# The last stage of a four-layer image kernel: its last block but one first, the last block stored in parts, and a fixed order

## The chip, the cores and the metric

The kernel runs on one core of a Trainium2 chip. The metric is the device time of one execution in microseconds (us), the median of three runs. The core has a matrix engine (TensorE, PE in the profile) with its weight loads (PEld), a vector engine (VectorE, DVE), a scalar engine (ScalarE, ACT), GpSimd (POOL) and a sync engine (SyncE, SP). Transfers between DRAM and the on-chip memory are issued as instructions of SP, ACT or POOL and carried out by 16 DMA engines. Each engine takes its instructions in the order in which they stand in its own queue; engines wait for each other, and for transfers, at semaphores.

## The reference

The input is an array of 8 images of 32 channels of 256 by 256, float32. Four layers follow each other, each of the form `x = x + layer(group_norm(x))`: a spectral convolution (FFT, 32 by 32 low modes mixed, inverse FFT), a 5 by 5 convolution, a gated recurrence over columns, and a mixing of directional maxima. The change touches the last two:

```python
# layer 2: a scan over the 256 columns; prev is the new column before, cur this column
r = sigmoid(r_i + r_h); z = sigmoid(z_i + z_h); n = tanh(n_i + r * n_h)
new = n * z + cur * (1.0 - z)
# layer 3: running maxima from four sides, then one matrix over 5*32 channels
x_con = concatenate((x, cummax_down, cummax_up, cummax_right, cummax_left), axis=1)
out = einsum('bchw,oc->bohw', x_con, W) + b
```

`_gn` ahead of each layer needs the mean and variance over a whole image, so layer 3's scales are known only when the recurrence has ended. One of the four maxima runs against the direction of the recurrence, so layer 3 goes through the columns from the last to the first.

## The kernel before

The program is four stages, one function each. The first two (`forward_and_mix`, `inverse_and_conv`) do layers 0 and 1 and leave their result in DRAM as `x2d`.

**The recurrence** (`recurrence`, lines 684 to 906) works on 32 blocks of 8 columns. A column is done in two half steps (`step(w, x)`, x = 0 and 1), four images each, so that one half step's matrix products run while the other's gates are computed. A half step has its matmuls on PE (lines 753 and 761), three sigmoids and a tanh on ACT (828, 830, 831, 835), four operations on DVE (829, 834, 840 and 842, the last writes the new column `hs`), and two on POOL (837, `zm` times `cur`, and 843, which adds the new column to the raw block `xw`). Between line 835 and line 840 one piece of extra work on DVE is fitted in (line 839): a running maximum from the left (`fm`, line 864) or a statistic (`bst`, line 875). As soon as a block is ended its `xw` is stored to DRAM as `x3d` by eight DMAs of 256 KB from SP (`store`, line 849), and its `fm`, when the pieces are through, as `fwd` by eight more. The `fwd` of the last block, 31, is issued from POOL instead of SP. Each of these DMAs reads 32 partitions. At the end lines 902 to 906 turn the statistics into `mv3`.

**The last stage** (`maxima_and_mix`, lines 909 to 1059) first makes its constants: it turns `mv3` into scales (`finish_stats`, lines 63 to 71, with a power on POOL), scaled weights `wsc` (936, 938) and biases `bres` (961, 962), and fills `cuts` and `top` (967 to 972) and `wsum` (942 to 946). A scheduler places this part: the fills and `wsum`, which need no statistics, stand on DVE in block 2 of the recurrence. Then it goes through blocks 31 to 0 in an order written out by hand (`tc.manual_schedule`). For a block it loads `x3` (the `x3d` block, 2 MB) and `fw` (the `fwd` block, 2 MB) from SP (line 980), with two buffers each, one block ahead. DVE does seven operations of maxima within the columns (lines 1014 to 1026: `x`, `top`, the scans `dq` and `uq`, and three times `m`) and, between them, eight steps of the maximum from the right (`back(7)` to `back(0)`, line 1012), each from the one before, across blocks by way of `after`. PE mixes five sources into eight banks (`mix`, line 1043: x, fw, the `downs` made of `m` and `dq`, the `ups` made of `uq` and `m`, then `rv`), ACT adds the bias (1058) and stores each half block (1059). `m`, `dq` and `uq` have one buffer each.

Instructions of different stages share each engine's queue. A tile of the last stage that lies in on-chip memory used by the recurrence waits until that memory's last user there is done.

Of the kernel before, what the change touches and what calls it, by code (L numbers as in the profile page):

```python
# [9 lines left out]
F32 = mybir.dt.float32  # L10
# [6 lines left out]
P = 128  # L17
# [3 lines left out]
EPS = 1e-5  # L21
# [662 lines left out]
def recurrence(tc, k, d, x2d, x3d, fwd, stb, first, loaded, mean1, mv3):  # L684
# [10 lines left out]
    with ExitStack() as ctx:  # L695
        one = ctx.enter_context(tc.tile_pool(name="bc", bufs=1))
        blk = ctx.enter_context(tc.tile_pool(name="bb", bufs=2))
# [22 lines left out]
        def load(bi):  # L720
            if bi:
                t = blk.tile([P, B, WB, Q], F32, name=f"xw_{bi}", tag="xw", bufs=4)
                for b in range(B):
                    nc.sync.dma_start(out=t[:, b], in_=columns(x2d, b, bi * WB, (bi + 1) * WB))
            else:
                t = first
                nc.sync.dma_start(out=t[:, B - 1], in_=columns(x2d, B - 1, 0, 8))
            raws[bi] = t
            norms[bi] = blk.tile([P, B, WB, Q], F32, name=f"xn_{bi}", tag="xn")
# [119 lines left out]
        def store(bi, dst, t):  # L849

            for a in range(A):
                for b2 in range(2):
                    (nc.gpsimd if bi == NB - 1 and dst is fwd else nc.sync).dma_start(
                        out=dst[bi, :, a, b2].rearrange("(i c) n -> c i n", c=C),
                        in_=t[rows(a), 4 * b2 : 4 * b2 + 4].rearrange("p i w q -> p i (w q)"),
                    )
# [13 lines left out]
        def finish(bi):  # L870
            raw = raws[bi]
            store(bi, x3d, raw)
            for b in range(B):
                pieces[1].append(
                    lambda b=b: nc.vector.bn_stats(bst[:, b, bi, :], raw[:, b].rearrange("p w q -> p (w q)"))
                )

        with tc.manual_schedule(engines=None):
# [5 lines left out]
            for bi in range(NB):  # L884
                for wi in range(WB):
# [7 lines left out]
                    running(bi, wi)  # L893
                finish(bi)
# [4 lines left out]
        parts = bst.rearrange("p b n (h k) -> p b (n h) k", k=3)  # L899
        n = 2 * NB  # L900
        second = one.tile([P, B, n], F32, name="second")
        nc.vector.tensor_tensor(second, parts[:, :, :, 1], parts[:, :, :, 1], ALU.mult)
        nc.vector.scalar_tensor_tensor(second, parts[:, :, :, 2], n / float(W * Q), second, ALU.mult, ALU.add)
        nc.vector.tensor_reduce(mv3[:, :, 0], parts[:, :, :, 1], AX.X, ALU.add)
        nc.vector.tensor_reduce(mv3[:, :, 1], second, AX.X, ALU.add)
        nc.vector.tensor_scalar_mul(mv3, mv3, 1.0 / n)


def maxima_and_mix(tc, k, d, x3d, fwd, mv3, mean1, out):
# [4 lines left out]
    NB = W // WB  # L914
    with ExitStack() as ctx:
        one = ctx.enter_context(tc.tile_pool(name="cc", bufs=1))
        blk = ctx.enter_context(tc.tile_pool(name="cb", bufs=2))
        op = ctx.enter_context(tc.tile_pool(name="co", bufs=3))
        ps = ctx.enter_context(tc.tile_pool(name="cp", bufs=2, space=PSUM))
# [5 lines left out]


        sta, _ = finish_stats(tc, one, ps, k, mv3, B, k.pair, "c", "o1", 2)
        st = one.tile([P, 2, 2], F32, name="st3")
        for i in range(4):
            q = slice(32 * i, 32 * i + 32)  # L930
            nc.vector.tensor_copy(st[q], sta[q, i::4, :])
        shift = one.tile([P, 2], F32, name="shift3")
        nc.vector.scalar_tensor_tensor(shift, st[:, :, 0], -1.0, st[:, :, 1], ALU.mult, ALU.mult)
        wsc = one.tile([P, 2, 5, C], F32, name="wsc")
        for b2 in range(2):
            nc.vector.tensor_scalar_mul(wsc[:, b2], w3, st[:, b2, 1:2])

            nc.vector.tensor_tensor(wsc[:, b2, 0], wsc[:, b2, 0], k.ident32, ALU.add)


        wsum = one.tile([P, A, C], F32, name="wsum")
        nc.vector.tensor_tensor(wsum[:, 0], w3[:, 0], w3[:, 1], ALU.add)
        for t in range(2, 5):
            nc.vector.tensor_tensor(wsum[:, 0], wsum[:, 0], w3[:, t], ALU.add)
        for j in range(1, A):
            nc.vector.tensor_copy(wsum[:, j], wsum[:, 0])
        sel = one.tile([P, 2, 4], F32, name="sel")
        nc.vector.memset(sel, 0.0)
        for i in range(4):
            q = slice(32 * i, 32 * i + 32)  # L950
            nc.vector.tensor_copy(sel[q, :, i], shift[q])
        bp = ps.tile([P, 2, 4], F32, name="bp", tag="o0")
        nc.tensor.matmul(
            bp.rearrange("p b i -> p (b i)"),
            lhsT=wsum.rearrange("p j o -> p (j o)"),
            rhs=sel.rearrange("p b i -> p (b i)"),
            start=True,
            stop=True,
        )
        bres = one.tile([P, 2, 4], F32, name="bres")  # L960
        nc.vector.tensor_scalar_add(bres, bp, b3[:, 0:1])
        nc.vector.tensor_tensor(bres, bres, mean1.rearrange("p (b i) -> p b i", b=2), ALU.add)


        QP = Q + 2
        cuts = one.tile([P, 2, 2 * WB, QP], F32, name="cuts")
        nc.vector.memset(cuts, BIG)
        nc.vector.memset(cuts[:, 0, :, 0:1], -BIG)
        nc.vector.memset(cuts[:, 1, :, QP - 1 : QP], -BIG)
        cutf = cuts.rearrange("p s w q -> p s (w q)")  # L970
        top = one.tile([P, 2, WB, QP], F32, name="top")
        nc.vector.memset(top, -BIG)

        xs = {}

        def load(bi):

            for src, tag, n in ((x3d, "x3", A + 2), (fwd, "fw", A)):
                t = xs[bi, tag] = blk.tile([P, n, 2, WB, Q], F32, name=f"{tag}_{bi}", tag=tag)
                nc.sync.dma_start(out=t[:, 0:A].rearrange("p a b w q -> p (a b) (w q)"), in_=src[bi].rearrange("p a b n -> p (a b) n"))  # L980
# [10 lines left out]
        after = None  # L991
        with tc.manual_schedule(engines=None):
            load(NB - 1)
            for bi in range(NB - 1, -1, -1):
                if bi > 0:
                    load(bi - 1)
                xt, fw = xs.pop((bi, "x3")), xs.pop((bi, "fw"))
                rev = blk.tile([P, A, 2, WB, Q], F32, name=f"rv_{bi}", tag="rv")
                x = [xt[:, a] for a in range(A)]

                m = blk.tile([P, 6, 2, WB, Q], F32, name=f"m_{bi}", tag="m", bufs=1)
                dq = blk.tile([P, 2, WB, QP], F32, name=f"dq_{bi}", tag="dq", bufs=1)
                uq = blk.tile([P, 2, WB, QP], F32, name=f"uq_{bi}", tag="uq", bufs=1)
                tt = nc.vector.tensor_tensor
                df, uf, tf = (t.rearrange("p b w q -> p (b w q)") for t in (dq, uq, top))

                def back(w):
                    last = after if w == WB - 1 else rev[:, :, :, w + 1, :]
                    if last is None:
                        nc.vector.tensor_copy(rev[:, :, :, w, :], xt[:, 0:A, :, w, :])  # L1010
                    else:
                        tt(rev[:, :, :, w, :], last, xt[:, 0:A, :, w, :], ALU.max)  # L1012

                tt(flat(xt[:, A : A + 2]), flat(xt[:, 0:A:2]), flat(xt[:, 1:A:2]), ALU.max)
                back(7)
                tt(top[:, :, :, 1 : 1 + Q], xt[:, A], xt[:, A + 1], ALU.max)
                back(6)
                nc.vector.tensor_tensor_scan(df, cutf[:, 0], tf, -BIG, ALU.min, ALU.max)  # L1018
                back(5)
                nc.vector.tensor_tensor_scan(uf[:, ::-1], cutf[:, 1, ::-1], tf[:, ::-1], -BIG, ALU.min, ALU.max)  # L1020
                back(4)
                tt(rows_of(m[:, 2:4]), twice(dq[:, :, :, 0:Q]), rows_of(xt[:, 0 : A + 1 : A]), ALU.max)  # L1022
                back(3)
                tt(rows_of(m[:, 0:2]), twice(uq[:, :, :, 2 : 2 + Q]), rows_of(xt[:, A - 1 : A + 2 : 2]), ALU.max)  # L1024
                back(2)
                tt(flat(m[:, 4:6]), flat(m[:, 1:4:2]), flat(xt[:, 1:3]), ALU.max)  # L1026
                back(1)
                back(0)
                after = rev[:, :, :, 0, :]
                downs = [m[:, 2], m[:, 3], m[:, 5], dq[:, :, :, 1 : 1 + Q]]  # L1030
                ups = [uq[:, :, :, 1 : 1 + Q], m[:, 4], m[:, 1], m[:, 0]]

                fws, rvs = [fw[:, a] for a in range(A)], [rev[:, a] for a in range(A)]
                pts = [
                    [ps.tile([P, 2 * H], F32, name=f"o_{bi}_{b2}_{i}", tag=f"o{i}") for i in range(4)] for b2 in range(2)
                ]


                def mix(b2, t, src, first=False, last=False):
                    for j in range(A):  # L1040
                        for i in range(4):
                            q = slice(32 * i, 32 * i + 32)
                            nc.tensor.matmul(  # L1043
                                pts[b2][i][32 * j : 32 * j + 32].rearrange("p (w q) -> p w q", q=Q),
                                lhsT=wsc[q, b2, t, :],
                                rhs=src[j][q, b2],
# [153 lines left out]
```

## Time and profile before

| what | value |
|---|---|
| median of 3 runs | 3066.25 us (3065.99 to 3067.99) |
| the profiled execution's own time | 3069.01 us |
| its span, first to last instruction | 3067.2 us |
| busy share PE, DVE, ACT, POOL | 91%, 84%, 61%, 28% |
| mean granted TensorE clock | 0.956 |
| last `hs` of the recurrence starts | 2402.73 us |
| first DVE operation on block 31 of the last stage starts | 2431.40 us |

The times of the profile count from the start of the span. In the page's slices each digit is the busy share of an engine in one of 40 equal pieces of the span (76.7 us each), so the recurrence ends in the 32nd digit. A timeline row gives start and duration in us, engine, line, operation and tiles (written `out<-in`), and in brackets the idle time before it with what ended it. A windows row gives a stretch, its length, and for each engine the busy us and, in brackets, the number of instructions, then the granted clock, the share of time in which the DMA engines were busy, and GB/s.

### The profile page before, as it was taken

To read this page: it belongs to the slowest core of one execution; us is meant where nothing else is said; L and a number is where in the kernel's file an instruction comes from. 1 tells how busy PE (TensorE), PEld (TensorE's weight loads), DVE (VectorE), ACT (ScalarE), POOL (GpSimd) and SP (SyncE) were. 2 spreads that over 40 slices of the span, in tenths; PEclk is the share of its full clock that TensorE was granted. 3 is DMA by queue.
4 is the path that set the end of the run, shared out by engine and by line. 5 is a ranking of instruction groups with operands and counts; after the bars stand their busy time and mean duration, and the time that the engine had idled before them with its cause. 6 is when DMAs were issued, how large, how long until landed. Compare 5 with 4: busy or idle time off the path is not lost.

```text
span 3067.2 us, 111686 instructions
## 1 busy us (share of the span) xinstructions
PE 2796.5 (91%) x47736; PEld 1645.3 (54%) x47736; DVE 2585.2 (84%) x5178; ACT 1870.4 (61%) x4482; POOL 858.2 (28%) x1247
## 2 busy tenths in 40 slices
PE   7986799999999799999999999999999588888887
PEld 4665344444444466666666666666666233333333
DVE  5752587778888589999999999999999799999997
ACT  3432377676777578888888888888887222222222
POOL 0110011111111355555555555555555200000000
PEclk9985899999999899999999999999999799999998
DMA  9977577777775565667666676666764588888885
GB/s 385 392 283 222 154 230 225 218 224 219 231 221 165 146 148 139 142 158 167 148 142 141 154 167 151 144 142 149 167 157 115 180 327 329 328 330 329 330 327 226
DMA packets 468193, 655.69 MB, mean 214 GB/s; under 512 B 328784, under 2 KB 329696, under 8 KB 441456
## 3 DMA queue, kind: packets, MB, share of 16 engines
q1 hardware_dynamic: 407528, 487.89, 54.6%
q0 software_dynamic: 16784, 84.11, 8.4%
q10 hardware_dynamic: 43384, 76.55, 6.9%
q8 instruction: 374, 6.13, 0.8%
q14 instruction: 123, 1.01, 0.1%
HBM read 371.63 MB, written 272.63 MB: 210 GB/s over the span
## 4 chain that ended last, share of the span: by engine, by line
PE 69%; DVE 20%; DMA 5%; issue 3%; ACT 2%; SPq 0%; ACTq 0%; POOL 0%; DVEq 0%; POOLq 0%
PE r L753 14%; PE z L753 13%; PE vp L487 11%; PE ni L753 6%; PE nh L753 6%; PE up L418 4%; DVE rv L1012 4%; PE yp L131 3%; DMA spec<-smd 3%; DVE dq L1018 2%; DVE uq L1020 2%; DVE m L1026 2%; DVE m L1024 2%; DVE m L1022 2%; PE sp L158 2%
## 5 line engine op out<-in xcount | busy, mean ns | idle before, releaser
L761 PE MATMUL z<-hs,weights 64*64 64x256 f32 x4080 | 539.2, 382 | 0.0
L761 PE MATMUL ni<-hs,weights 64*64 64x256 f32 x4080 | 525.7, 375 | 0.0
L761 PE MATMUL r<-hs,weights 64*64 64x256 f32 x4080 | 525.0, 375 | 0.0
L843 POOL TENSOR_TENSOR xw<-xw,hs 128x256 f32<-128x256 f32 x496 | 340.2, 686 | 635.3 <-DVE hs L842 635.3
L1058 ACT ACTIVATE ot<-o,bres 128x512 f32<-128x512 f32 x256 | 155.1, 688 | 505.1 <-PE o L1043 489.7
L487 PE MATMUL vp<-x,c_conv 64*64 64x384 f32 (+5 forms) x4608 | 428.8, 491 | 4.9 <-DVE x L520 4.9
L520 DVE SCALAR_TENSOR_TENSOR x<-vp,r,x 128x128 f32<-128x128 f32 (+2 forms) x640 | 350.6, 563 | 87.9 <-PE vp L487 75.1
L837 POOL TENSOR_TENSOR a<-zm,xn 128x256 f32<-128x256 f32 x510 | 373.1, 732 | 7.0 <-ACT zm L830 6.7
L835 ACT ACTIVATE n<-n,bih 128x256 f32<-128x256 f32 x510 | 259.5, 509 | 186.4 <-DVE n L834 186.4
L1043 PE MATMUL o<-m,wsc 32*32 32x512 f32 x3072 | 228.8, 724 | 108.0 <-DVE m L1026 104.4
L753 PE MATMUL r<-hs,weights 64*64 64x256 f32 x2040 | 318.9, 389 | 4.4 <-DVE hs L842 3.4
L753 PE MATMUL z<-xn,weights 64*64 64x256 f32 x2040 | 305.8, 377 | 14.9 <-DMA xw<-x2d 14.9
L487 PEld LDWEIGHTS vp<-x,c_conv 64*64 64x64 f32 x4608 | 222.4, 132 | 180.0 <-issue 104.4
L753 PE MATMUL r<-xn,weights 64*64 64x256 f32 x2040 | 305.3, 376 | 2.1 <-ACT rs L828 2.1
L753 PE MATMUL nh<-xn,weights 64*64 64x256 f32 x2040 | 306.2, 377 | 0.0
L753 PE MATMUL z<-hs,weights 64*64 64x256 f32 x2040 | 305.3, 376 | 0.0
L753 PE MATMUL ni<-hs,weights 64*64 64x256 f32 x2040 | 305.1, 375 | 0.0
L733 ACT ACTIVATE xn<-xw,shift,turned 128x256 f32<-128x256 f32 x496 | 290.3, 586 | 0.0
L829 DVE SCALAR_TENSOR_TENSOR n<-nh,bhh,rs 128x256 f32<-128x256 f32 x510 | 246.2, 483 | 46.4 <-ACT rs L828 32.6
L761 PEld LDWEIGHTS ni<-hs,weights 64*64 64x64 f32 x4080 | 284.8, 133 | 0.3
L761 PEld LDWEIGHTS r<-hs,weights 64*64 64x64 f32 x4080 | 280.9, 131 | 0.2
L828 ACT ACTIVATE rs<-r,brz 128x256 f32<-128x256 f32 x510 | 241.7, 474 | 54.2 <-PE r L761 33.8
(162 smaller groups left out, 6230.3 us busy)
## 6 DMA issues: line engine op xcount, KB each, us to landing
xb<-in_xl_dram POOLq DMA_DIRECT2D x96, 768.0 KB, 7.6
xa<-in_xt_dram SPq DMA_DIRECT2D x64, 1024.0 KB
x<-x3d SPq DMA_DIRECT2D x32, 2048.0 KB
fw<-fwd SPq DMA_DIRECT2D x32, 2048.0 KB
out_dram<-ot ACTq DMA_DIRECT2D x64, 1024.0 KB
xw<-x2d SPq DMA_DIRECT2D x248, 256.0 KB
fwd<-fm SPq DMA_DIRECT2D x248, 256.0 KB
x3d<-xw SPq DMA_DIRECT2D x248, 256.0 KB
```

The costliest lines, as they stand in the source:

```text
L487: ins = nc.tensor.matmul(vps[bank][to, :, dst], lhsT=k.conv[r, P : P + 64] if kind == 2 else k.conv[r, o], rhs=pair_of(u, ch, g, lo, hi, s ...
L520: nc.vector.scalar_tensor_tensor(x, src[o], r1[rows, g : g + 1], x, ALU.mult, ALU.add, accum_out=s1[rows, 0, n, ch, g : g + 1])
L733: nc.scalar.activation(norms[bi][:, b, w], raws[bi][:, b, w], AF.Identity, bias=shift[:, b : b + 1], scale=sc[:, 1, b : b + 1])
L753: ins = nc.tensor.matmul(out[r], lhsT=weights[r, kind, gate, :], rhs=src[r], start=start, stop=stop)
L761: ins = nc.tensor.matmul(out[pairs[1 - i]], lhsT=weights[r, kind, gate, :], rhs=prev[r, :, q0 : q0 + Q], start=False, stop=stop,)
L828: rs = nc.scalar.activation(r, p["r"], AF.Sigmoid, bias=brz[:, 0:1])
L829: nc.vector.scalar_tensor_tensor(m, p["nh"], bhh[:, 2:3], r, ALU.add, ALU.mult)
L835: nc.scalar.activation(m, m, AF.Tanh, bias=bih[:, 2:3])
L837: product = nc.gpsimd.tensor_tensor(a, zm, cur, ALU.mult)
L843: nc.gpsimd.tensor_tensor(raw, raw, new, ALU.add)
L1043: nc.tensor.matmul(pts[b2][i][32 * j : 32 * j + 32].rearrange("p (w q) -> p w q", q=Q), lhsT=wsc[q, b2, t, :], rhs=src[j][q, b2], start=first,
L1058: nc.scalar.activation(ot[:, i], pts[b2][i], AF.Identity, bias=bres[:, b2, i : i + 1])
```

## The change

What it does, part by part:

1. **Last block but one first.** The last stage takes block 30's within-column maxima first, block 31's next. `load_x(30)` is issued by ACT's queue; every other load stays on SP. `known(bi)` (PE's first four sources) and `finish(bi)` (the fifth source, biases, stores) are now separate, and an explicit order of DVE's work for the two blocks is given; `m10` stands for the first maximum of block 30, `b07` for `back(7)` of block 31. The right-hand maximum still runs 31, then 30. A copy `edge` is added for block 29, since the `rv` of block 30 and 29 share a buffer.
2. **Pools.** `x3`, `rv` and the recurrence's `xw` get a pool per buffer, so that block 30's `x3` buffer can lie in memory that is free before the recurrence ends.
3. **Last block stored in three parts.** `x3d` of block 31 is stored as columns 0 to 3 after column 3, 4 and 5 after column 5, and 6 and 7 at the end: 24 DMAs instead of eight. `fwd` of block 31 is issued by SP behind them.
4. **No scheduling freedom.** The statistics and the constants stand in `manual_schedule`; the fills and `wsum` go from DVE to POOL (`constants`).

In the built program of the changed kernel the instructions stand as follows. On ACT, `load_x(30)` is behind the third sigmoid of half step (250, 0), column 250 and x = 0, and waits for the eight `x3d` stores of block 30. On DVE, `m10` is in half step (250, 1), right behind line 829's operation there, and waits for that load. On POOL, the fills stand between the last half step of column 15 and the product of (16, 0), and `wsum` between that product and the next addition. The rest of the order is that of the text below. On SP, `load_x(31)` and `load_f(30)` come behind all stores of block 31, then `load_f(31)`, then `load_x(29)`. `m02` waits for PE's last read of `dq` of block 30, `m03` for that of `uq`, `m04` for that of `m`; `load_x(29)` waits for `b10`.

```diff
@@ recurrence
-                t = blk.tile([P, B, WB, Q], F32, name=f"xw_{bi}", tag="xw", bufs=4)
+                t = xws[(bi - 1) % 4].tile([P, B, WB, Q], F32, name=f"xw_{bi}", tag="xw")
...
-        def store(bi, dst, t):
+        def store(bi, dst, t, lo=0, hi=WB):
...
-                    (nc.gpsimd if bi == NB - 1 and dst is fwd else nc.sync).dma_start(
-                        out=dst[bi, :, a, b2].rearrange("(i c) n -> c i n", c=C),
+                    nc.sync.dma_start(
+                        out=dst[bi, :, a, b2, lo * Q : hi * Q].rearrange("(i c) n -> c i n", c=C),
...
-            store(bi, x3d, raw)
+            store(bi, x3d, raw, 6 if bi == NB - 1 else 0)
...
+                    if bi == NB - 1 and wi in (3, 5):
+                        store(bi, x3d, raws[bi], wi - 3 if wi == 3 else 4, wi + 1)
@@ maxima_and_mix
+        def constants():
+            nc.gpsimd.memset(cuts, BIG)
...
+            nc.gpsimd.memset(top, -BIG)
+            nc.gpsimd.memset(sel, 0.0)
+            nc.gpsimd.tensor_tensor(wsum[:, 0], w3[:, 0], w3[:, 1], ALU.add)
...
+        def load_x(bi, queue):
+            xs[bi] = xps[slot(bi)].tile([P, A + 2, 2, WB, Q], F32, name=f"x3_{bi}", tag="x3")
+            queue.dma_start(
...
+        def back(bi, w):
+            if w == WB - 1:
+                if bi == NB - 3:
+                    nc.vector.tensor_copy(edge, rvs[bi + 1][:, :, :, 0, :])
...
+        with tc.manual_schedule(engines=None):
+            load_x(NB - 2, nc.scalar)
+            load_x(NB - 1, nc.sync)
+            constants()
+            sums()
+            order("m10")
+            variance()
+            order("m11 m12")
+            scales()
+            load_f(NB - 2)
+            load_f(NB - 1)
+            order("m13")
+            biases()
+            order("m14 m15 m16")
+            known(NB - 2)
+            order("m00 b07 m01 b06 b05 m02 b04 b03 m03 b02 b01 b00")
+            order("b17 b16 b15 b14 b13 b12 b11 b10")
+            finish(NB - 2)
+            load_x(NB - 3, nc.sync)
+            load_f(NB - 3)
+            order("m04 m05 m06")
+            known(NB - 1)
+            finish(NB - 1)
+            for bi in range(NB - 3, -1, -1):
...
```

From block 29 on, the order within a block is that of before.

## The prediction

> **What bounds the kernel now.** I read the page's slices first, then the chain of waits in order of time around the end of the recurrence, then timelines and windows there. Slices (DVE's busy tenths, then TensorE's granted clock):
>
> ```profile
> DVE  5752587778888589999999999999999799999997
> PEclk9985899999999899999999999999999799999998
> ```
>
> DVE is nearly full in the recurrence (digits 16 to 31) and in the last stage (33 to 40). Only the 32nd digit, the passage between them, has a hole. The chain of waits there:
>
> ```profile
> 2402.73 0.43 DVE hs L842
> ...
> 2410.59 12.31 DMA x3d<-xw
> 2423.11 8.07 DMA x<-x3d
> 2431.40 2.29 DVE x L1014
> ```
>
> The recurrence ends, the stores of block 31 take until 2423.11, its load until 2431.40, and only then DVE starts on the last stage. From then on DVE alone sets the pace, as the timeline of DVE shows for two blocks:
>
> ```profile
> 2450.52 2.29 DVE L1014 TENSOR_TENSOR x<-x 128x2048 f32<-128x2048 f32 x1
> 2469.91 2.28 DVE L1014 TENSOR_TENSOR x<-x 128x2048 f32<-128x2048 f32 x1
> ```
>
> A block takes 19.39 us. Block 29 begins at 2469.91, and from there the change leaves DVE's work alone but for `edge`. So the question is at what time block 29 begins. The change puts two instructions into the recurrence, at these places of the timelines (ACT, then DVE):
>
> ```profile
> 2371.82 0.47 ACT L831 ACTIVATE zs<-z,brz 128x256 f32<-128x256 f32 x1
> ...
> 2374.19 0.49 DVE L829 SCALAR_TENSOR_TENSOR n<-nh,bhh,rs 128x256 f32<-128x256 f32 x1
> 2374.78 0.42 DVE L834 TENSOR_TENSOR n<-ni,n 128x256 f32<-128x256 f32 x1
> ...
> 2376.31 0.42 DVE L842 TENSOR_TENSOR hs<-n,a 128x256 f32<-128x256 f32 x1
> ```
>
> The first row is the sigmoid behind which ACT issues the load of block 30, the second the operation behind which `m10` stands: 2.4 us lie between. What the DMA engines do then, and at other times, in windows (last columns: clock, DMA share, GB/s):
>
> ```profile
> 2372.00:2374.00 2.00, 2.00 (x44) 1.42 (x39) 1.86 (x5) 1.12 (x3) 0.85 (x2) 1.00 0.95 226
> 2374.00:2376.00 2.00, 2.00 (x40) 1.30 (x36) 1.85 (x5) 1.40 (x4) 1.38 (x2) 1.00 0.91 246
> 2378.00:2380.00 2.00, 2.00 (x40) 1.26 (x36) 1.89 (x4) 1.48 (x4) 0.58 (x2) 1.00 0.77 182
> ...
> 2405.00:2406.00 1.00, 0.00 (x0) 0.00 (x0) 1.00 (x3) 0.00 (x0) 1.00 (x2) 0.97 0.94 203
> 2406.00:2407.00 1.00, 0.00 (x0) 0.00 (x0) 1.00 (x3) 0.00 (x0) 1.00 (x3) 0.50 0.98 205
> 2428.00:2430.00 2.00, 0.00 (x0) 0.00 (x0) 0.00 (x0) 0.00 (x0) 0.00 (x0) 0.50 1.01 434
> ```
>
> The engines are busy with the `fwd` stores of block 30 until 2380. Stores run at 200 to 250 GB/s, loads at 430. And the clock halves two us after PE's last matmul (2404.2).
>
> **What the Trainium skill says.** "DMA: Bandwidth & Descriptors", Queues, rings and completion order: each DMA engine takes turns between the queues that have work for it, and Issuing engines are not separate DMA queues: a second issuing queue saves issue time alone. So ACT's load will share with SP's stores; no window of before has a load from one queue beside 32-partition stores from another. "SBUF — State Buffer", Door 1: the DMA port swizzle: 32 partitions reach 8 of 16 ports, about 218 GB/s; the windows agree (203 and 205 against 434). "TensorE: Matmul & The Clock Gate", Architectural detail: VectorE's queue is strict first in, first out; so what stands behind `m10` waits with it. The same page, What's actually happening: an idle PE falls to half clock within some 3.4 us and needs as long, busy, to come back. The trace agrees on the fall; the return took 8.7 us (2431.4 to 2440.1) and 4.4 (2449.3 to 2453.7).
>
> **Part 1, `m10` in the recurrence: a loss.** ACT gets to the load at 2372.3, when the `x3d` stores of block 30, issued until 2368.0, have about landed. First data comes about 0.5 us after an issue (load of 2450.67: 213 GB/s in the window from 2451), so near 2373. By the windows 1.56 MB of stores are left then. The load is 2.10 MB. If both move at 170 GB/s (340 together, my estimate between the 328 of load and store mixed over 2460 to 2480 and the 430 of loads alone), the stores end after 9.2 us with 0.54 MB of the load left, 1.3 us at 430: 2383.4, with 0.5 to complete 2383.9. Ends: 2378.4 if the load goes first (4.9 us at 430), 2385.6 if the stores do. `m10` then runs, and DVE goes on 2.2 us later, at 2386.1 in place of 2374.78: 11.3 us (5.8 to 13.0). Behind `m10` stand line 834 and all of DVE's recurrence, so hs of (250, 1), then PE of (251, 1). DVE has next to no slack to win this back. PE stands still from about 2377 to 2388 and goes cold. A half step is 2.65 us (hs at 2376.31, at 2402.73 ten later), PE works through nearly all of it, and at half clock it takes some 4.9: one such half step costs 2.3 (bounds 0 and 4.6, two of them). The recurrence ends **13.6 us later** (5.8 to 17.6).
>
> **Part 2, constants on POOL: nothing, net.** On DVE they cost the recurrence this: six half steps from hs at 1120.68 to hs at 1140.48 took 19.80 us against 15.87. On POOL the fills (DVE rows: 1.82, 0.94, 0.07 twice) hold up the product of (16, 0) by about 3.1, and `wsum`, seven small operations, (16, 1) by about 0.9: 4.0 against 3.9. No trace shows a large fill on POOL; at twice the time it costs 5 us more, hidden in POOL's idle 1.1 to 1.4 us per half step it saves 1.5. I take 0.
>
> **Part 3, stores in parts and `fwd` on SP.** All times from here are in the frame of before; the 13.6 is added at the end. Two thirds of the extra DMA issues lie in the recurrence, where SP waits anyway. After the last step 0.52 MB of `x3d` and 2.10 MB of `fwd` are left in place of 4.19 MB. The issues of the eight small ones at 0.4 us (the first rows of before: 0.30, 0.42, 0.58) last until 2407.2, `fwd` at 210 GB/s until 2417.2. `load_x(31)` comes at 4.9 us later, `load_f(30)` at another 4.9, with some of the queueing of before: **2428.8**. Ends: 2426.8 if the engines alone set it (2.62 MB from 2404.3 at 215), 2432.7 if the issues do (eight at 0.67, eight at 1.28, then the 12.6 us that `fw` took from 2423.50 to 2436.09).
>
> **Part 4, DVE's new order.** `mv3` is there at 2412.66 as before, the variance at 2414.31. Then m11 1.14 and m12 2.27, under which POOL's power (1.67) hides: 2417.7. Scales 2.1, m13 2.27, biases 0.4, m14 to m16 at 2.20: 2429.1. m00, b07, m01, b06, b05 (2.20, 0.34, 1.13, twice 0.65): 2434.1. Now m02 must wait for PE's reads of `dq`: PE has x from 2420.6 (64 matmuls in 4.08 at half clock), waits for `fw` until 2428.8, does it in 4.1, and `downs` in some 3.2: 2436.1, a wait of 2.0. Then m02, b04, b03, m03, three and eight steps (2.27, 1.3, 2.27, 1.9, 5.2): 2449.0. `load_x(29)` is issued only now; the load of 2450.67 was through by about 2457.3, 6.7 us, and I add 0.6 for the stores of block 30: 2456.3. DVE has m04 to m06 (6.6) to do meanwhile; 0.7 stays open. Block 29 begins at 2456.3 in place of 2469.91; the copy `edge` takes back 0.34: **13.3 us gained** (9.4 with `fw` at 2432.7; 15.3 without the wait at m02). The load of x3 of block 28 I cost at nothing: ahead of it are x3 and `fw` of 29 and the store of 30, with itself 8.4 MB, 22 us at 381 GB/s (the steady part's 328 at a share of 0.86), so it is there by 2471.5, and due at 2475.7; if it is late, its lateness adds.
>
> **Sum.** 13.6 - 13.3 + 0 = +0.3 us. Against the profiled execution's 3069.01 us (span 3067.2) that is 3069.3; the median lies 2.8 under it: **3067 us**.
>
> **Rivals.**
> - *The load is served ahead and PE stays warm.* The delay is 5.8, the gain 13.3: 3059 us. For it: the engines take turns, and loads run at twice the stores' pace. Against it: two queues of stores at 2405 to 2412 gave no more than 202 to 217, and PE fell cold in two us. It decides below a delay of 7.2.
> - *Slower: the clock stays low.* One mechanism: after the standstill PE, halved, holds up each half step by 2.3 us until the clock returns. Four half steps make 3066.25 + 11.3 + 9.2 - 13.3 = 3073.5 us; it decides from about 3.5 on. For it: the 8.7 us of before. Against it: that is under two half steps at 4.9, and the other return took 4.4.
> - *A wait takes the place of the one removed:* `fw` of block 30 comes at 2432.7, m02 waits 5.9, the gain is 9.4: 3070.5 us, within the noise. For it: the issue times of before. Against it: a quarter of `x3d` is left.
>
> **How the numbers follow.** Forecast 0.50, first rival 0.20, clock 0.18, late `fw` 0.12. A measurement here can tell about 0.2% (6.1 us) from no change. Faster 0.20; slower 0.18 and 0.02 for a late `fw` with slow fills on POOL; same 0.60. The range 3058 to 3075 takes in half of the first rival, the end values of part 1 and the clock rival at four half steps. The forecast's own range is 3062 to 3072.
>
> **What would show it.** In the profile after: DVE idle near 2375 for some 9 us until DMA `x<-x3d`, in front of the first row of `m10`; a dip of the clock behind it; the last hs near 2416; then DVE busy from the last hs on without the hole of 12 us, a wait for PE of some 2 us ahead of the scan of block 31, one under 1 us ahead of block 29. Wrong if `m10` finds its data (faster), if the clock stays at half for over 10 us, or if DVE waits for x3 of block 28.

## The result, and the profile after

The changed kernel takes 3072.39 us (median of 20 runs, 3067.18 to 3083.11) beside 3068.80 us of the kernel before on the same chip: a ratio of 1.0013 with a 95% interval of 1.0005 to 1.0022. That is 1.5 to 6.8 us slower, about 4.0 us, less than the 0.2% that I had set as the bound. The forecast was 3067 us with +0.3 us of change. That the change would stay within 0.2% was right; the sum was about 3.7 us too low; and the mechanism of its largest term was wrong, as the runs below show.

The profiled execution of the changed kernel took 3070.90 us (span 3069.1). The slices show the same picture as before; DVE's hole at the 32nd digit is smaller (8 for 7), and the 31st, the end of the recurrence, has fallen from 9 to 8; the clock's row is too coarse to tell of the change:

```profile
DVE  5753588888878589999999999999998899999997
...
PEclk9985799999999899999999999999999799999998
```

The timelines of ACT and DVE around the load of block 30, the counterpart of the lines of before, show the standstill (the bracket is the idle time ahead of an instruction and what ended it; lines have moved by two, so line 834 is now 836 and 842 is 844):

```profile
2368.82 0.36 ACTq L1004 DMA_DIRECT2D x<-x3d  x1
...
2370.90 0.48 DVE L831 SCALAR_TENSOR_TENSOR n<-nh,bhh,rs 128x256 f32<-128x256 f32 x1
2380.36 2.29 DVE L1040 TENSOR_TENSOR x<-x 128x2048 f32<-128x2048 f32 x1 [8.98 <-DMA x<-x3d]
2382.57 0.42 DVE L836 TENSOR_TENSOR n<-ni,n 128x256 f32<-128x256 f32 x1
...
2388.77 0.48 DVE L831 SCALAR_TENSOR_TENSOR n<-nh,bhh,rs 128x256 f32<-128x256 f32 x1 [1.46 <-ACT rs L830]
```

`m10` (L1040) waits 8.98 us for the load, and DVE goes on 11.67 us after the start of L831 in place of 0.59: **11.1 us** of standstill. The last row is the price of the cold TensorE (its clock at half): one wait of 1.46 us. The windows show the clock (last columns: clock, DMA share, GB/s) fall and return:

```profile
2374.00:2376.00 2.00, 0.00 (x0) 0.00 (x0) 0.00 (x0) 0.00 (x0) 0.00 (x0) 1.00 0.86 278
2378.00:2380.00 2.00, 0.00 (x0) 0.00 (x0) 0.00 (x0) 0.00 (x0) 0.00 (x0) 0.50 0.99 389
...
2386.00:2388.00 2.00, 2.00 (x28) 1.19 (x24) 1.28 (x3) 0.00 (x0) 0.61 (x1) 0.54 0.00 0
2388.00:2390.00 2.00, 2.00 (x44) 1.38 (x40) 1.13 (x3) 1.39 (x4) 0.80 (x2) 1.00 0.27 66
```

The chain of waits from the end of the recurrence to block 29 (start, duration, what) has lost the stores of 12.31 us and the load of 8.07 us behind them. In their place stand SP's issues, two loads and PE:

```profile
2424.45 1.17 SPq L1004
2425.80 14.76 DMA fw<-fwd
2440.69 6.90 PE o L1067 x130
2447.61 2.36 DVE dq L1050
...
2461.47 8.41 DMA x<-x3d
2469.91 2.29 DVE x L1040
```

DVE waits twice on this way, 3.79 us for PE at 2447.61 and 1.79 us for x3 at 2469.91. Block 29 begins at 2469.91, in this profile at the very time it began at before.

**How to compare two executions.** That equality is chance. The hs operations are a clock for it: taken one by one, those of the changed kernel begin 2.5 us earlier than those of before at the start of the recurrence (1046.15 against 1048.66), ahead of every instruction that the change moves, and 3.28 us earlier at (250, 0). In the executions of the kernels below, the point (250, 0) lies anywhere from 5.4 us earlier to 7.5 us later. So I read two differences that are free of it: the *loss in the recurrence* (shift of the last hs less the shift ahead of the standstill) and the *passage* (from the last hs to the start of block 29).

| | before | after | change |
|---|---|---|---|
| loss in the recurrence | | 9.30 + 3.28 | +12.6 |
| passage, last hs to block 29 | 2469.91 - 2402.73 = 67.2 | 2469.91 - 2412.03 = 57.9 | -9.3 |
| block 29 (with `edge`) | 19.4 | 19.9 | +0.5 |
| sum | | | +3.8 |

The sum of 3.8 us agrees with the measured 4.0 us. (Of the 1.9 us by which the spans of the two profiles differ, 1.2 are PE's work after DVE's last instruction, 8.12 us against 6.89; it took 6.92 in a later execution of the same changed kernel, so this difference comes and goes from one execution to the next.)

### The profile page after: what moved, and what is told of

The parts are those of the page before. It is cut to its first block, busy times and chain, and to the rows that moved or that the text cites. A ratio compares the mean times of both kernels' runs of the same rounds, so it can differ in the third digit from the quotient of the medians.

```text
span 3069.1 us, 111691 instructions
## 1 busy us (share of the span) xinstructions
PE 2790.3 (91%) x47736; PEld 1645.5 (54%) x47736; DVE 2583.7 (84%) x5167; ACT 1868.8 (61%) x4482; POOL 858.7 (28%) x1251
## 4 chain that ended last, share of the span: by engine, by line
PE 69%; DVE 20%; DMA 5%; issue 3%; ACT 1%; SPq 1%; POOL 0%; ACTq 0%; DVEq 0%; POOLq 0%
PE r L755 14%; PE z L755 13%; PE vp L487 12%; PE ni L755 6%; PE nh L755 6%; PE up L418 4%; DVE rv L1035 4%; PE yp L131 3%; DVE dq L1050 2%; DVE uq L1052 2%; DVE m L1061 2%; DVE m L1058 2%; DVE m L1055 2%; PE o L1067 2%; PE sp L158 2%
## 5 line engine op out<-in xcount | busy, mean ns | idle before, releaser
L755 PE MATMUL r<-hs,weights 64*64 64x256 f32 x2040 | 319.8, 390 | 15.3 <-DVE hs L844 14.4
L1067 PE MATMUL o<-m,wsc 32*32 32x512 f32 x3072 | 221.7, 705 | 99.6 <-DVE m L1061 96.8
L831 DVE SCALAR_TENSOR_TENSOR n<-nh,bhh,rs 128x256 f32<-128x256 f32 x510 | 246.2, 483 | 47.7 <-ACT rs L830 33.6
```

What stands on the lines that cost most here:

```text
L755: ins = nc.tensor.matmul(out[r], lhsT=weights[r, kind, gate, :], rhs=src[r], start=start, stop=stop)
L831: nc.vector.scalar_tensor_tensor(m, p["nh"], bhh[:, 2:3], r, ALU.add, ALU.mult)
L1067: nc.tensor.matmul(banks[bi][b2][i][32 * j : 32 * j + 32].rearrange("p (w q) -> p w q", q=Q), lhsT=wsc[q, b2, t, :], rhs=src[j][q, b2], st ...
```

## The experiments

All are edits of the changed kernel; in the cuts of code, `...` marks lines left out. The ratios are to the kernel before on the same chip; the changed kernel itself stands at 1.0013 and, repeated at the end, at 1.0022.

| run | median us | ratio (95%) | loss in the recurrence | passage |
|---|---|---|---|---|
| late | 3060.74 | 0.9976 (0.9967 to 0.9985) | 0.0 | 57.6 |
| backfirst | 3069.34 | 0.9999 (0.9986 to 1.0011) | 12.2 | 52.4 |
| both | 3058.82 | 0.9963 (0.9950 to 0.9976) | 0.2 | 54.7 |
| alone | 3071.44 | 1.0004 (0.9992 to 1.0016) | 11.1 | 57.6 |
| mid | 3057.64 | 0.9972 (0.9964 to 0.9980) | 1.9 | 52.4 |
| whole | 3076.85 | 1.0031 (1.0022 to 1.0040) | 12.8 | 61.6 |
| fwfirst | 3072.12 | 1.0024 (1.0016 to 1.0032) | 12.0 | 57.1 |
| dveconst | 3073.97 | 1.0024 (1.0016 to 1.0033) | 14.0 | 58.7 |
| again | 3077.98 | 1.0022 (1.0009 to 1.0034) | 12.6 | 57.3 |
| both2 | 3059.08 | 0.9960 (0.9945 to 0.9975) | 1.2 | 54.7 |
| mid2 | 3057.67 | 0.9955 (0.9937 to 0.9972) | 1.9 | 52.4 |
| dveconst2 | 3073.32 | 1.0009 (0.9998 to 1.0020) | 12.4 | 58.5 |

### Without m10 in the recurrence (late)

```
-            order("m10")
             variance()
-            order("m11 m12")
+            order("m10 m11 m12")
```

> The changed kernel with m10 placed behind the variance instead of inside the recurrence; the load of block 30 stays where it is. Theory (the standstill is on the path): the recurrence ends 12.4 us earlier against its own course (11.1 of standstill and 1.3 of cold clock), DVE has 2.2 us more in the passage, and the wait for PE ahead of the scan of block 31 shrinks from 3.8 to about 1.6 us, since the transfer of fw behind it does not depend on DVE: about 12 us faster than the changed kernel, 3060 to 3061 us. From the last hs to block 29 it stays at 57.9 us. Rival (the passage is bound by something that m10 in the recurrence takes off the path): the passage grows by 5 us or more and less than 7 us are gained.

Measured: 0.9976, which is 0.37% or 11.4 us under the changed kernel. The loss in the recurrence is gone, the passage stays at 57.6 us. Its waits are as expected, one a little shorter:

```profile
DVE x L1040 <- DMA x<-x3d: 2.1, 1, 2.1
...
DVE dq L1050 <- PE o L1067: 0.8, 1, 0.8
```

These are two of DVE's four waits from the last hs to block 29 (total us, times, longest); the others, 0.9 and 0.8 us around the last sums, are there in every version. The 2.2 us of `m10` were paid out of the wait for PE, which fell from 3.8 to 0.8. So the standstill was on the path with nearly all of its length (11.4 us by the times, 12.6 in the trace), and the rival, a passage that takes the gain back, is out.

### The backward steps ahead of the scans (backfirst), and both edits (both)

```
-            order("m00 b07 m01 b06 b05 m02 b04 b03 m03 b02 b01 b00")
-            order("b17 b16 b15 b14 b13 b12 b11 b10")
+            order("m00 b07 m01 b06 b05 b04 b03 b02 b01 b00")
+            order("b17 b16 b15 b14 b13 b12 b11 b10 m02 m03")
```

> The changed kernel with the two scans of block 31 moved behind all sixteen backward steps. Theory (the two waits of the passage can be covered by DVE's own work): the wait for PE (3.8 us) and the wait for x3 of block 29 (1.8 us) both go, since the last backward step comes 8.3 us earlier and the load of block 29 with it: 57.9 us from the last hs to block 29 become 52.3, and the whole is 5.6 us faster than the changed kernel, about 3067 us. Rival (PE or the transfers set the pace there): the waits come back ahead of block 29 or of its first scan, and 2 us or less are gained.

> Both edits: m10 behind the variance, and the scans of block 31 behind the backward steps. Theory: no standstill in the recurrence, and no waits between the last hs and block 29 but the one for the sums: 57.9 - 5.6 + 2.2 = 54.5 us for the passage, the recurrence 12.4 us shorter: about 3072.4 - 12.4 + 2.2 - 5.6 = 3057 us, 12 us under the kernel before. Rival (the waits are not independent, the transfer of fw or PE comes to set the pace): 3060 us or more.

Measured: passages of 52.4 and 54.7 us, where 52.3 and 54.5 were expected, and ratios of 0.9999 and 0.9963. The timeline of DVE of the second shows both scans running without a wait behind the fifteen backward steps that are one group, and block 29 (the last row) without one either:

```profile
2438.99 10.86 DVE L1035 TENSOR_TENSOR rv<-rv,x 128x512 f32<-128x512 f32 x15
2449.77 2.35 DVE L1050 TENSOR_TENSOR_SCAN dq<-cuts,top 128x1056 f32<-128x1056 f32 x1
...
2461.00 2.28 DVE L1040 TENSOR_TENSOR x<-x 128x2048 f32<-128x2048 f32 x1
```

Ending the backward steps 8 us earlier (41.3 us after the last hs in backfirst, 49.4 in the changed kernel) does two things at once: it covers PE's reading of `dq`, and it frees the buffer of block 30 earlier, so that x3 of block 29 is there in time. Once DVE has other work there, neither PE nor the loads make it wait in the passage. The two edits together beat both kernels: 0.9963 is 11.4 us under before, 15.3 under the changed kernel by the ratios.

### The load without the stores beside it (alone)

The forecast put the length of the standstill down to sharing: the load was to have half of the DMA bytes until the `fwd` stores of block 30 had gone. Here those stores are left out, and the later load of `fw` of block 30 reads block 29's place:

```
-                if wi == WB - 1:
+                if wi == WB - 1 and bi != NB - 2:
                     store(bi, fwd, t)
```

> The changed kernel without the eight fwd stores of block 30 (2.1 MB left out; the later load of fw of block 30 reads block 29's place instead, so that the traffic of the passage is unchanged). Theory (the load is slow because it shares the DMA engines with these stores): it then takes about 0.5 us to begin, 4.9 us at 430 GB/s and 0.5 us to complete, lands some 5.9 us after its issue in place of 11.5, and DVE waits about 3.4 us in place of 9.0; with a shorter cold phase the whole is 5.6 to 7 us faster, 3065.5 to 3067 us. Rival (the load is slow by itself, because it reads what has just been written or because of ScalarE's queue): it still takes 9 us or more, and the time stays at 3070 to 3072 us.

Measured: a ratio of 1.0004, about 2.8 us under the changed kernel with an interval that also holds none. The timelines of ACT and DVE decide:

```profile
2370.48 0.35 ACTq L1004 DMA_DIRECT2D x<-x3d  x1
...
2379.39 2.29 DVE L1040 TENSOR_TENSOR x<-x 128x2048 f32<-128x2048 f32 x1 [6.46 <-DMA x<-x3d]
```

With no stores beside it, the load still takes 8.9 us from its issue to its use, in place of 11.5. I had expected 5.9, so the theory fails: sharing costs 2.6 us, not 5.6, and the load by itself is 3 us longer than my price. The rival (9 us or more, 3070 to 3072 us) is met all but exactly; its two reasons are taken up below. Where the 3 us go is in the windows of this run (last columns: clock, DMA share, GB/s):

```profile
2371.00:2372.00 1.00, 1.00 (x24) 0.76 (x20) 1.00 (x2) 0.47 (x2) 0.12 (x1) 1.00 1.24 229
2372.00:2373.00 1.00, 1.00 (x24) 0.51 (x16) 0.89 (x3) 1.00 (x3) 0.46 (x1) 1.00 0.34 131
2373.00:2374.00 1.00, 1.00 (x24) 0.77 (x20) 0.00 (x0) 0.14 (x1) 0.91 (x2) 1.00 0.96 410
...
2377.00:2378.00 1.00, 0.00 (x0) 0.00 (x0) 0.00 (x0) 0.00 (x0) 0.00 (x0) 1.00 0.27 98
2378.00:2379.00 1.00, 0.00 (x0) 0.00 (x0) 0.00 (x0) 0.00 (x0) 0.00 (x0) 1.00 0.04 16
```

The first packets begin at 2371.5, 1.0 us after the issue, not 0.5. The full rate comes only at 2373, 2.5 us after the issue; four us at about 400 GB/s follow; and a thin rest trickles until nearly 2379. The load of before that the prediction read its 0.5 us from (x3 of block 29, issued at 2450.67) starts in the same way:

```profile
2451.00:2452.00 1.00, 1.00 (x33) 0.69 (x32) 1.00 (x1) 0.00 (x0) 0.00 (x0) 0.50 1.15 213
2452.00:2453.00 1.00, 1.00 (x34) 0.26 (x3) 1.00 (x2) 0.00 (x0) 0.00 (x0) 0.50 0.40 131
2453.00:2454.00 1.00, 1.00 (x44) 0.71 (x31) 1.00 (x2) 0.00 (x0) 0.00 (x0) 0.64 0.78 328
```

Its packets begin at 2451.6, inside the first window; the prediction took the start of the window, and left out the next one, with 131 GB/s. That load is on SP's queue and reads what was stored more than 100 us earlier (its `x3d` stores were issued from 2316.8 to 2325.6). So the slow start comes neither from ScalarE's queue nor from reading what has just been written. Where the thin rest at the end comes from stays open. The Trainium skill, "DMA: Bandwidth & Descriptors", section Anatomy of one DMA, fits the time of one DMA (issued from GpSimd) by 2.0 us plus its bytes at 436 GB/s; for this load that is an estimate of 6.8 us, nearer than my 5.9, and the measured 8.9 is still 2.1 above it.

How the load and the stores share, the DMA queues of the changed kernel tell for 2371 to 2377.5 (queue: packets, MB, share of the 16 engines; q10 is ACT's queue, q1 is SP's):

```profile
q10 hardware_dynamic: 104, 1.70, 84.1%
q1 hardware_dynamic: 96, 0.19, 7.6%
```

Nearly as many packets of each went by, but those of the load hold 16.3 KB (1.70 MB / 104) and those of the stores 2.0 KB. That fits engines that take turns packet by packet, so that the load gets nine tenths of the bytes; I had let them share by bytes. The Trainium skill, "DMA: Bandwidth & Descriptors", Queues, rings and completion order, has the turns at packet granularity; the prediction drew on that section and left the unit out, and the count agrees with it. The turns are not the whole cost. The two together moved 1.91 MB in these 6.5 us, 294 GB/s where the prediction had 340, and a packet of the load took 0.84 us of its engine (84.1% of 16 engines over 6.5 us, by 104; from 2373 to 2377 alone it is the same). With no stores beside it, from 2373 to 2377 of this run, it took 0.60:

```profile
q10 hardware_dynamic: 101, 1.62, 94.6%
```

Why the packets get longer beside the stores no run here shows.

A shorter standstill also did not spare the clock: the standstill fell to 8.6 us, and the cold half steps behind it cost 2.6 us in place of 1.5, so that the loss in the recurrence is 11.1 against 12.6. PE was back at work at 2383.6 and the full clock at 2389.3, 5.7 us later; in the changed kernel these are 3.3 us apart (2384.6 and 2387.9).

### m10 later in the recurrence (mid)

`m10` gets a dependency on an operation at the end of half step (253, 1) (`k.mark`, noted in `step`), and in the trace it runs right behind that half step's `hs`. That is six half steps behind its place in the changed kernel; the backward steps stand first as in backfirst.

```
...
-                tt(flat(xt[:, A : A + 2]), flat(xt[:, 0:A:2]), flat(xt[:, 1:A:2]), ALU.max)
-                return
+                ins = tt(flat(xt[:, A : A + 2]), flat(xt[:, 0:A:2]), flat(xt[:, 1:A:2]), ALU.max)
+                return bi == NB - 2 and tc.add_manual_dep(ins.ins, k.mark, AFTER, reason="the load is through by then")
...
```

> m10 stays inside the recurrence, but six half steps further on, behind the last DVE operation of (253, 1), some 16 us after the load was issued; the scans of block 31 stand behind the backward steps as in the run with that edit alone. Theory (it was the wait, not the work, that cost the recurrence): no wait for the load, the recurrence ends 2.2 us later than its own course for the 2.2 us of work and nothing for the clock, the passage is 52.4 us: as the version with m10 behind the variance, within 1 us, about 3058 us, 11 us under the kernel before. Rival (VectorE has slack there and hides the work): the recurrence ends at most 0.5 us later, 3056 us. Second rival (any delay of VectorE there leaves TensorE cold): 4 us or more later.

Measured: 0.9972, no wait, and a loss of 1.9 us. The row of `m10` now stands between two rows of the recurrence without a bracket:

```profile
2390.55 0.43 DVE L844 TENSOR_TENSOR hs<-n,a 128x256 f32<-128x256 f32 x1
2390.89 2.29 DVE L1040 TENSOR_TENSOR x<-x 128x2048 f32<-128x2048 f32 x1
2393.10 0.48 DVE L831 SCALAR_TENSOR_TENSOR n<-nh,bhh,rs 128x256 f32<-128x256 f32 x1
```

So the work of `m10` costs the recurrence nearly its own 2.2 us, as VectorE has next to no slack there, and the other 10.7 of the changed kernel's 12.6 us were the wait and the cold clock behind it. Since the passage is 2.3 us shorter, it comes out where both does: the two intervals overlap.

### The stores in three parts undone (whole)

```
-            store(bi, x3d, raw, 6 if bi == NB - 1 else 0)
+            store(bi, x3d, raw)
...
-                    if bi == NB - 1 and wi in (3, 5):
-                        store(bi, x3d, raws[bi], wi - 3 if wi == 3 else 4, wi + 1)
```

> The changed kernel with x3d of block 31 stored whole at the end, as before, in place of three parts. Theory: 1.57 MB more stand ahead of the fwd stores and the three loads after the last step, 6.8 us at the 231 GB/s that the windows show there; x3 of block 31 and fw of block 30 land 6.8 us later, and the wait for PE ahead of the scan grows from 3.8 to about 10.6 us, partly split off as a wait of 2 us ahead of m00: 6 to 7 us slower than the changed kernel, about 3079 us. Rival (DVE's work on block 30 covers the stores anyway): within 1 us of the changed kernel.

Measured: 1.0031, 0.18% over the changed kernel with wide bounds; in the trace the passage is 3.7 us longer (61.6), and the wait for PE grew by 3.3 us, not by 6.8:

```profile
2455.73 2.36 DVE L1048 TENSOR_TENSOR_SCAN dq<-cuts,top 128x1056 f32<-128x1056 f32 x1 [7.13 <-PE o L1065]
```

PE begins with `fw` 31.8 us after the last hs, against 28.7. Direction right, size half: in the changed kernel the engines are not full behind the last step (66 GB/s from 2412 to 2416, 181 in the next 4 us, then 233), because SP issues the last stores one after the other there until 2424.3. Part of the bytes that were taken away had an idle place. So by the trace the three parts are worth 3.7 us, and this part of the change pays; the times, with intervals that touch (1.0022 to 1.0040 against 1.0005 to 1.0022), point the same way.

### fw ahead of x3 (fwfirst)

In the manual order, `load_x(NB - 1, nc.sync)` moves from the head to between `load_f(NB - 2)` and `load_f(NB - 1)`.

> The changed kernel with SP's loads in another order at the end: fw of block 30 ahead of x3 of block 31. Theory (the wait ahead of the scan is the transfer of fw and nothing else): fw lands about 5 us earlier, PE reads it from about 10 us before it does now at the latest rate of one load, and the wait of 3.8 us goes; x3 of block 31 lands later and makes m00 wait up to 1.5 us: 2.3 to 3.8 us faster than the changed kernel, about 3069 us. Rival (the loads share the engines, so the order doesn't matter, or PE at half clock sets the pace): 0.5 us or less.

Measured: 1.0024, no gain. The transfer did come 5.7 us earlier (PE begins with `fw` 23.0 us after the last hs), and the wait ahead of the scan is gone; but another stands 5 us ahead of the scan now:

```profile
2447.45 2.29 DVE L1040 TENSOR_TENSOR x<-x 128x2048 f32<-128x2048 f32 x1 [2.56 <-DMA x<-x3d]
```

That is `m00` of block 31, and together with 2.2 us of wait ahead of block 29 it leaves 0.8 us of gain in the passage. The first theory had the cause of the wait right and what is late next too small.

### The constants on VectorE again (dveconst, dveconst2), and the repeats

In `constants()` each `nc.gpsimd` becomes `nc.vector`.

> The changed kernel with its constants (cuts, top, sel, wsum) made by VectorE instead of GpSimd, as before. Theory (moving them was worth nothing net): within 1 us of the changed kernel, and the excess of the recurrence's half steps around them is about 4 us on either engine. Rival (the 3.3 us by which the recurrence of the changed kernel ran ahead in its profile come from this move): 3 us slower, about 3075 us.

> The changed kernel with its constants made by VectorE once more, beside the changed kernel itself. Theory (moving them was worth nothing): within 1 us of the changed kernel. Rival (the move saved what the recurrence ran ahead by in the first trace): 3 us slower than it.

> The changed kernel once more, beside the three others on one chip. Theory: 0.13% over the kernel before; in its trace a loss of 12 to 13 us in the recurrence (of it 10.5 to 12.5 the standstill), a passage of 57 to 59 us from the last hs to block 29, whatever time the work before the recurrence took.

> The version with m10 behind the variance and the scans of block 31 behind the backward steps once more. Theory: 15 to 16 us (0.5%) under the changed kernel of the same chip; no loss in the recurrence, a passage of 54.7 us. Rival (the earlier runs differed by chip): less than 10 us.

> The version with m10 six half steps further on in the recurrence and the scans of block 31 behind the backward steps once more. Theory: 2.0 us lost in the recurrence, a passage of 52.4 us, as far under the changed kernel as the version with m10 behind the variance, within 1 us. Rival (the earlier ratios, 0.9963 and 0.9972, differ for a cause): 2 us or more slower than that one.

Ratios of 1.0024 and 1.0009 beside 1.0013 and 1.0022: the first is about 3 us above the changed kernel, as the rival had it, the second, on one chip with it, 4 below; together no difference that can be seen. Over sixteen half steps around 1126 us, the kernels with the constants on GpSimd lose 0.2 to 1.1 us against before, those with the constants on VectorE 0.2 and 0.3. And the lead of 3.3 us of the first trace is not theirs: with the constants on VectorE the recurrence ran 5.4 us ahead of before in one execution, 7.5 behind in the other.

The repeats hold. The changed kernel again lost 12.6 us in the recurrence and took 57.3 for the passage, as expected (its standstill, 10.3, is just under the range given); both2 at 0.9960 and mid2 at 0.9955 lie 0.62% and 0.67% under the changed kernel's 1.0022 of the same chip, more than the 0.5% expected but within the intervals, which are about 0.3% wide. Which of the two versions is the faster the runs don't tell. In both2 the recurrence lost 1.2 us in a single wait of VectorE for ScalarE, which had itself waited 1.79 us for TensorE; why TensorE was late stays open.

## Why the prediction was right or wrong

- **Part 1, the standstill: the size right, the mechanism wrong.** 11.3 us were forecast and 11.1 measured; 10.3 to 12.3 in the six other executions with the same order there. But the number was luck: two errors cancel. "If both move at 170 GB/s" failed: the stores got a tenth of the bytes, not half, and sharing cost 2.6 us, not 5.6. "First data comes about 0.5 us after an issue", the full rate of 430 GB/s from then on and "with 0.5 to complete" failed too: the first data comes after 1.0 us, the full rate after 2.5, and the load alone needs 8.9 us, not 5.9. The row of 8.07 us for the load of block 31, in the chain that the prediction shows, had such a price. The first rival's premise, a load that is served ahead, was therefore nearly true, and it still did not give the rival's 3059 us, since its delay of 5.8 rested on the same short price.
- **The clock: right, a little high.** 2.3 us for one half step at half clock; 1.5 measured, 2.6 in the run without the stores. The second rival, four such half steps, did not occur: the clock is at half from some 2378 to 2388, and PE worked in only the last 3.3 us of these. With this the recurrence lost 12.6 us (forecast 13.6). One reading behind it was wrong: "the clock halves two us after PE's last matmul (2404.2)". In the trace of before PE has no matmul between 2400.8 and 2412.9:

```profile
2412.91 0.58 PE L63 MATMUL stat_c<-mv,c_pair 128*128 128x16 f32 x2 [12.09 <-DVE mv L906]
```

The clock fell at 2405.9, so 5.1 us after the last matmul; in the changed kernel it fell 3.8 us after (2373.8 to 2377.6). A standstill of 11 us is longer than either, so the forecast did not suffer; the first rival's "PE fell cold in two us" rests on this reading too.
- **Part 2, the constants: right within what can be told.** Nothing net was forecast; 0.2 to 1.1 us of loss is what the traces show, and the times show none.
- **Parts 3 and 4, the passage: here the sum failed.** 13.3 us were forecast with `edge`, 8.8 came (9.3 less 0.5). Shifted by 9.30 into the frame of before, DVE was on time up to the end of m14 to m16 (2429.4, forecast 2429.1). Then PE got `fw` at 2431.4, not 2428.8. Of these 2.6 us, 0.8 lay in the stores, whose last packet ended at 2418.0 in place of 2417.2. The rest is the step "`load_x(31)` comes at 4.9 us later, `load_f(30)` at another 4.9": with its 1.8 for queueing it gave the two loads 11.6 us, and they took 13.4. It priced them by their bytes again; how much of the 1.8 us is their slow start, and how much the third load that was queued behind and moved along with them, the runs don't separate. The wait for PE became 3.8 in place of 2.0 us; with 0.4 of small things ahead of it the scan began 2.2 late. The rest up to b10 took 13.8 in place of 12.9, the eleven steps being 0.72 each. And x3 of block 29 took 8.4 us from issue to use, not 7.3, so its wait was 1.8 in place of 0.7. Together 4.3 us late at block 29 and 0.2 more for `edge`.
- **The third rival, `fw` late at 2432.7,** was nearer than my own step: 2431.4 lies between, and its gain of 9.4 is close to the 8.8 measured. It had got 0.12.
- **"DVE waits for x3 of block 28"** did not occur: DVE had no wait behind block 29.

In short: one price, the time from a load's issue to its use, was too low at three places. At the first a wrong share made up for it; at the other two it did not, and that is most of the 4 us. The 3067 us of the forecast is near the measured time because its largest loss was right by chance.

## What to carry to other kernels

Take a load's price from issue to first use in the trace, whole, and not as bytes over the full rate plus a bit: for the 2.1 MB loads here it was 8.1 to 8.9 us where the bytes alone, at 430 GB/s, take 4.9. An instruction that waits for such a load belongs behind as much other work of its engine as the load lasts; the same 2.2 us of `m10` cost 12.6 us at one place of the recurrence, and 1.9 six half steps later. And when a wait is to be covered, look first for work of the same engine that depends on nothing (the backward steps) before the transfers are re-ordered: the one gave 5.5 us of passage, the other 0.8.

## What the runs showed of the hardware that I had not expected

- A 2.1 MB load with the DMA engines to itself: first packets 1.0 us after the issue, full rate 2.5 us after it, DVE started 8.9 us after it.
- A load of 16.3 KB packets beside stores of 2.0 KB packets from another queue: 104 packets against 96 in 6.5 us, 1.70 MB against 0.19 MB, and 0.84 us for a packet of the load in place of 0.60 without the stores.
- The work before the recurrence differs by up to 13 us between single executions (start of the recurrence from 1044.0 to 1057.0 us), several times the effect studied. Differences within one stage, read off the same two instructions, were steady to 1 or 2 us (the standstill 10.3 to 12.3, the passage of the changed order 57.3 to 58.7).
